# Window attention, depthwise and quantised convolutions: band matrices by DMA, weights quantised beside the first bands, halved sums of exponentials, projections one step later

## The chip, the cores and the metric

The kernel runs on one core of one Trainium2 chip. The metric is the device time of one execution in microseconds. TensorE (PE in the profile) multiplies, ScalarE (ACT) applies functions, VectorE (DVE) and GpSimd (POOL) work elementwise, and SyncE (SP) issues the DMAs. Each engine works through its own instructions in order.

## The reference

Two layers on `x` of 4 x 128 channels x 128 x 128, all in float32. Layer 0 cuts each image into 9 x 9 overlapping windows of 16 x 16 pixels (step 14), and runs attention with 4 heads of 32 channels in each:

```python
y = _ln(tok, ln1_g, ln1_b)
q, k, v = split(y @ w_qkv)                       # per head
attn = softmax(q @ k.T * hd ** -0.5)
tok = (attn @ v) @ w_out + b_out + tok
merged = scatter_add(tok) / count                # back to the image, overlaps averaged
y = _ln(xf, ln2_g, ln2_b) @ w_p0 + b_p0          # 128 -> 256 channels
ym = depthwise_conv5x5(y, dw_k)                  # 256 channels, padding 2
ym = gelu(gelu(batchnorm(ym)))
x1 = ym @ w_p2 + b_p2 + xf
```

Layer 1 is a residual block with quantised activations (4 bits, 0 to 1) and quantised weights (4 bits, scaled by the largest absolute weight):

```python
out = conv3x3(act_quant(x1), weight_quant(w1)); out = batchnorm(out)
out = conv3x3(act_quant(out), weight_quant(w2)); out = batchnorm(out)
return out + x1
```

## The kernel before

**Preparation.** Weights are loaded, and the gains and biases of the layer norms are folded into them. Lines 165 to 196 bound the largest attention score from the weights and set `flag`; a second, safe version of all layers runs only if `flag` is set, which it is not here. Lines 202 to 224 load both 3x3 weights, find the largest absolute value (VectorE, then a reduction over partitions on POOL) and write them as fp8. Lines 229 to 279 make the matrices of the depthwise convolution. The 5x5 convolution runs on TensorE as a product over 40 rows (20 image rows by even and odd pixels) with a banded matrix per channel, in three shifts `s` and 32 outputs `m`. For each of the 96 pairs of shift and output, VectorE copies a picked pattern twice (L264), TensorE multiplies it with the taps (L269), and VectorE and ScalarE copy the result into `wst` (L277, L275). Eight DMAs store `wst` in `dw_d` (L279), from which the loop loads 768 KB a time into `w` (L471).

**Band loop.** A band is 16 image rows of one image; there are 9 an image, 36 in all (t = 0 to 35). The order of TensorE, ScalarE and VectorE is the order in which the program is written; SP and POOL are ordered by the scheduler. For band t the loop runs over its 9 regions j (windows side by side). `scores(j)`: 8 products into `sc` (L561), and two exponentials into `pt` (L569). Then `values(j-1)`: 8 products of `pt` with `v`, and 8 with a block of `ones`, which gives the sums of the exponentials in the same shape (L615); VectorE takes the reciprocal (L628) and multiplies (L630, L632); POOL adds the seam between regions (L635). A float32 product counts as two passes in the profile, so the 16 products are 32 passes.

**Side work.** `beside(t)` writes a list of steps for each band, which is laid evenly between the regions, a half of a region at a time, with `values_in(j)` (L549) between the halves:
- `one`, the layer norm and q/k projections of band t+1, four chunks of 4, 4, 4 and 2 rows (4 in the first band of an image). A chunk has four steps: head (centring product L306, square L308), tail (variance product L313, `rstd` L315 and L316, `xn` on VectorE L318, copy to `yr` on POOL L378), and the projections to q and k (L382).
- `two`, the output side of band t-1, four chunks with five steps: project (product with `wo` L420, `xf` on VectorE L423), head, tail, and the two products with `wp0` (L437) whose results go to `y2_d` (L451). Before the first of them, `post_begin` averages the seams on POOL (L404, L405, L407).
- convolution steps of an earlier half image, 16 for each of 8 units; four go beside a band where there are any. A step is 96 passes (L496), two copies on ScalarE (L505), four statistics on VectorE (L507) and four stores to `cv_d` (L511).

In `beside`, the index c counts the chunks, and chunk c of `one` stands beside chunk c of `two`. All PSUM tiles of the side work come from `ps_m`, three banks; `po` has one.

**After the loop.** Half an image of convolution is left, then the batch norm's statistics (L746 on), the Gelu and first 3x3 convolution pass, a second pass, and a last pass that writes the output.

Of the kernel before, what the change touches and what calls it, by code (L numbers as in the profile page):

```python
# [8 lines left out]
F32 = mybir.dt.float32  # L9
# [5 lines left out]
P = 128  # L15
# [17 lines left out]
CW = P // 2 + 2  # L33
NCK = 8
# [7 lines left out]
def layers(  # L42
# [47 lines left out]
    dw_d = dram.tile([NCK, P, 16 * 3 * 32], F32, name="dw_d")  # L90
# [37 lines left out]
    bng, bnb = vector(bn_g, "bng"), vector(bn_b, "bnb")  # L128
    wp2 = const.tile([P, 2, P], F32, name="wp2")
    nc.sync.dma_start(out=wp2, in_=w_p2.rearrange("(h p) m -> p h m", p=P))  # L130
    bp2 = vector(b_p2, "bp2")
    ga1, be1 = vector(gamma1, "ga1"), vector(beta1, "be1")
    ga2, be2 = vector(gamma2, "ga2"), vector(beta2, "be2")

# [4 lines left out]
    with (  # L139
# [25 lines left out]
        if not safe:  # L165


            sq = prep.tile([P, 2 * P], F32, name="sq")
            nc.vector.tensor_tensor(sq, wqkv[:, : 2 * P], wqkv[:, : 2 * P], ALU.mult)
            all1 = prep.tile([P, P], F32, name="all1")  # L170
            nc.vector.memset(all1, 1.0)
            pn = ps_p.tile([P, 2 * P], F32, name="pn")
            nc.tensor.matmul(pn, all1, sq, start=True, stop=True)
            norm = prep.tile([P, 2 * HEADS], F32, name="norm")
            nc.vector.tensor_reduce(
                norm, pn.rearrange("p (h d) -> p h d", d=HD), AX.X, ALU.add
            )
            mask = prep.tile([P, HEADS], F32, name="mask")
            nc.vector.tensor_reduce(
                mask, ident.rearrange("p (h d) -> p h d", d=HD), AX.X, ALU.add  # L180
            )
            qb2 = prep.tile([P, 1], F32, name="qb2")
            nc.vector.tensor_tensor(qb2, qb, qb, ALU.mult)
            nc.vector.tensor_scalar(mask, mask, qb2, None, ALU.mult)
            pq = ps_p.tile([P, HEADS], F32, name="pq")
            nc.tensor.matmul(pq, all1, mask, start=True, stop=True)

            bound = prep.tile([P, HEADS], F32, name="bound")
            nc.vector.tensor_scalar(bound, norm[:, :HEADS], float(P), None, ALU.mult)
            nc.vector.tensor_tensor(bound, pq, bound, ALU.add)  # L190
            nc.vector.tensor_tensor(bound, bound, norm[:, HEADS:], ALU.mult)
            top = prep.tile([P, 1], F32, name="top")
            nc.vector.tensor_reduce(top, bound, AX.X, ALU.max)
            nc.vector.tensor_scalar(
                flag, top[0:1, :], MAX_SCORE**2 / (2.0 * P), None, ALU.is_ge
            )

    wq, kscale = [], []
    with tc.tile_pool(name=f"wprep_{tag}", bufs=2) as wprep:
        for n, w in enumerate((w1, w2)):
            wf = wprep.tile([P, 9 * P], F32, name="wf")
            nc.sync.dma_start(out=wf, in_=w)
            am = wprep.tile([P, 1], F32, name="am")
            nc.vector.tensor_reduce(am, wf, AX.X, ALU.max, apply_absolute_value=True)
            alpha = wprep.tile([P, 1], F32, name="alpha")
            nc.gpsimd.partition_all_reduce(alpha, am, P, bass_isa.ReduceOp.max)  # L210
            nc.vector.tensor_scalar(alpha, alpha, 1e-12, None, ALU.add)
            ks = const.tile([P, 1], F32, name=f"kscale{n}")
            nc.vector.tensor_scalar(ks, alpha, 1.0 / 105.0, None, ALU.mult)
            ra = wprep.tile([P, 1], F32, name="ra")
            nc.vector.reciprocal(ra, alpha)
            nc.vector.tensor_scalar(wf, wf, ra, 1.0, ALU.mult, ALU.min)
            nc.vector.tensor_scalar(wf, wf, -1.0, 7.0, ALU.max, ALU.mult)
            nc.vector.tensor_scalar(wf, wf, ROUND, None, ALU.add)
            q = const.tile([P, 9, P], F8, name=f"wq{n}")
            nc.vector.tensor_scalar(  # L220
                q.rearrange("p t o -> p (t o)"), wf, ROUND, None, ALU.subtract, saturate=False
            )
            wq.append(q)
            kscale.append(ks)

# [3 lines left out]
    with (  # L231
        tc.tile_pool(name=f"dwp_{tag}", bufs=1) as dwp,
        tc.tile_pool(name=f"ps_w_{tag}", bufs=4, space=PSUM) as ps_w,
    ):
        zero = dwp.tile([P, 2 * 2 * 2 * CW], F32, name="zero")
        nc.gpsimd.memset(zero, 0.0)
        for b in range(B):
            for d in (y2_d[b][0][0:2], y2_d[b][NU - 1][UR + 2 :]):
                nc.sync.dma_start(
                    out=d.rearrange("r e c x -> (r e c x)").rearrange("(p n) -> p n", p=P), in_=zero  # L240
                )
        dwk = dwp.tile([P, 2, N_TAPS], F32, name="dwk")
        nc.sync.dma_start(out=dwk, in_=dw_k.rearrange("(h p) o i j -> p h (o i j)", p=P))
        pk = ps_w.tile([P, 2 * P], F32, name="pw")
        for h in range(2):
            nc.tensor.transpose(pk[:N_TAPS, h * P : (h + 1) * P], dwk[:, h, :], ident)
        taps = dwp.tile([N_TAPS, 2 * P], F32, name="taps")
        nc.vector.tensor_copy(taps, pk[:N_TAPS])

        pick = dwp.tile([N_TAPS, 35, 7], F32, name="pick")  # L250
        nc.gpsimd.memset(pick, 0.0)
        for k in range(N_TAPS):
            dy, dx = divmod(k, 5)
            nc.vector.tensor_copy(pick[:, dy + 15, dx + 1 : dx + 2], ident[:N_TAPS, k : k + 1])
        wst = dwp.tile([P, NCK, 16, 3, 32], F32, name="wst")
        ms = [dwp.tile([N_TAPS, 2, 32, 2], F32, name=f"m{n}") for n in range(4)]
        for m in ms:
            nc.gpsimd.memset(m, 0.0)
        for n in range(3 * 32):
            s, ro, eo = n // 32, n % 32 // 2, n % 2  # L260
            m = ms[n % 4]
            for half in range(2):

                nc.vector.tensor_copy(  # L264
                    m[:, half, : GR + 4, :],
                    pick[:, 15 - ro : 15 - ro + GR + 4, 2 * s - eo + 1 : 2 * s - eo + 3],
                )
            pw = ps_w.tile([P, 2 * P], F32, name="pw")
            nc.tensor.matmul(pw, m.rearrange("t a r e -> t (a r e)"), taps, start=True, stop=True)  # L269
            for half in range(2):  # L270
                hs = slice(64 * half, 64 * half + 64)
                o = wst[hs, :, :, s, 2 * ro + eo]
                i_ = pw[hs].rearrange("p (k a c) -> p k a c", k=NCK, a=2)[:, :, half, :]
                if half:
                    nc.scalar.copy(o, i_)  # L275
                else:
                    nc.vector.tensor_copy(o, i_)  # L277
        for k in range(NCK):
            nc.sync.dma_start(out=dw_d[k], in_=wst[:, k].rearrange("p c s m -> p (c s m)"))  # L279
# [7 lines left out]
    with ExitStack() as actx:  # L287
# [6 lines left out]
        small = pool("small", 6)  # L294
        ps_s, ps_o, ps_m = (pool(n, k, space=PSUM) for n, k in (("ps_s", 1), ("ps_o", 1), ("ps_m", 3)))

        xb, yr, qs, kr, ob = {}, {}, {}, {}, {}

        def normalise(src, n):
# [11 lines left out]
            def tail():  # L311
                pv = ps_m.tile([P, 512], F32, name="pm")
                nc.tensor.matmul(pv[:, :n], avg, held["sq"][:, :n], start=True, stop=True)  # L313
                rstd = work.tile([P, 512], F32, name="rstd")
                nc.scalar.activation(rstd[:, :n], pv[:, :n], AF.Ln, bias=eps_t)  # L315
                nc.scalar.activation(rstd[:, :n], rstd[:, :n], AF.Exp, scale=-0.5)  # L316
                xn = work.tile([P, 512], F32, name="xn")
                nc.vector.tensor_tensor(xn[:, :n], src(), rstd[:, :n], ALU.mult)  # L318
                return xn
# [143 lines left out]
        def conv_steps(n):  # L463
# [4 lines left out]
            def load(k):  # L468
                ut = up.tile([P, 4, 16, CW], F32, name="u")
                wt = up.tile([P, 16, 3, 32], F32, name="w")  # L470
                nc.sync.dma_start(out=wt.rearrange("p c s m -> p (c s m)"), in_=dw_d[k])  # L471
                for half in range(2):
                    ch = 32 * k + 16 * half
                    for a, z in ((0, GR), (GR, GR + 4)):
# [12 lines left out]
            def pair(k, jj):  # L487
                ut, wt = U[k]
                pc = [ps_m.tile([P, 2, 256], F32, name="pm") for _ in range(2)]
                for j in range(2):  # L490
                    for s in range(3):
                        for half in range(2):
                            hs = slice(64 * half, 64 * half + 2 * GR + 8)
                            for q in range(4):
# [5 lines left out]
                                    wt[hs, c, s, :], ut[hs, :, c, s : s + 64],  # L500
# [30 lines left out]
        def attention(t):  # L531
# [39 lines left out]

            def scores_safe(j):
# [35 lines left out]
            def values(j):  # L608
                pt, v = S.pop(("pt", j)), S.pop(("v", j))
                po = ps_o.tile([P, 2, NT], F32, name="po")  # L610
                for m in range(1 if safe else 2):
                    for kc in range(2):
                        for h in range(HEADS):
# [19 lines left out]
                if j:  # L633
                    seam = o[:, :, j * STEP : j * STEP + 2]
                    nc.gpsimd.tensor_tensor(seam, seam, part, ALU.add)  # L635

            begin()
            return scores_safe if safe else scores, values_in, values

        def beside(t):  # L640

# [328 lines left out]
```

## Time and profile before

| | us |
|---|---|
| median of 3 runs (4049.6 to 4061.1) | 4058.78 |
| the profiled execution: time | 4057.53 |
| the profiled execution: span, first to last instruction | 4055.7 |
| first attention scores start | 168.6 |
| second band's scores start | 217.5 |
| the band loop ends | about 2830 |
| last unit of the convolution | 2830 to 2985 |

All views come from one profiled execution. A group's row reads: line, engine, operation, output from input, shapes, count; then busy time in us and the mean duration of one in ns; then the idle time of the engine just before them and what ended it. A timeline's row gives start and duration in us. A wait's row reads: engine, line, what it waited for, total us, number, longest.

### The profile page before, as it was taken

How to read it: one execution, taken by the hardware profiler on the slowest of the kernel's cores; microseconds unless marked ns; L12 is line 12 of the kernel's file. 1: busy time of each engine (PE TensorE's matmuls, PEld its weight loads, DVE VectorE, ACT ScalarE, POOL GpSimd, SP SyncE). 2: the span in 40 equal slices, each digit the busy share in tenths (PEclk: the TensorE clock that was granted, in tenths of full speed). 3: DMA queues.
4: the chain of work that ended last, by engine and by line, in shares of the span. 5: the costliest groups of instructions: out<-in, count | busy, mean ns of one | idle time of the engine just before them, and what ended most of it. 6: DMA issues, size and time to landing. Idle time of an engine off the chain costs nothing.

```text
span 4055.7 us, 87210 instructions
## 1 busy us (share of the span) xinstructions
PE 3762.9 (93%) x35916; PEld 1914.1 (47%) x35916; DVE 1826.5 (45%) x3358; ACT 2326.4 (57%) x3534; POOL 384.2 (9%) x1381
## 2 busy tenths in 40 slices
PE   7699999999999999999999999997688889999999
PEld 5355455555555555555545555553333333334444
DVE  5244444444444444444444444442245555685433
ACT  3367666666666666666666666653156667662233
POOL 0011110111110010111110111100011111100000
PEclk9999999999999999999999999998579999999999
DMA  1223266676656657655666764657888889760487
GB/s 39 108 62 80 73 135 149 146 143 152 148 116 141 148 134 159 150 140 110 150 147 139 160 146 118 144 129 162 182 255 300 295 297 304 231 199 1 137 271 250
DMA packets 782938, 643.68 MB, mean 159 GB/s; under 512 B 572736, under 2 KB 585664, under 8 KB 782528
## 3 DMA queue, kind: packets, MB, share of 16 engines
q1 hardware_dynamic: 782528, 637.98, 60.8%
q8 instruction: 286, 4.69, 0.5%
q14 instruction: 124, 1.02, 0.1%
HBM read 365.07 MB, written 272.76 MB: 157 GB/s over the span
## 4 chain that ended last, share of the span: by engine, by line
PE 76%; DMA 9%; ACT 4%; issue 3%; DVE 3%; POOL 2%; SPq 2%; ACTq 0%; POOLq 0%; DVEq 0%
PE po L615 14%; PE pc L787 12%; PE pm L496 9%; PE sc L561 8%; PE pm L306 6%; PE pm L382 6%; PE pm L313 6%; PE pm L437 5%; DMA cv<-cv_d 3%; PE pm L549 3%; PE pb L849 3%; PE pm L420 2%; PE pw L269 2%; DMA c1l<-c_d 2%; DMA u<-y_d 2%
## 5 line engine op out<-in xcount | busy, mean ns | idle before, releaser
L628 DVE RECIPROCAL rd<-po 128x256 f32<-128x256 f32 x324 | 569.6, 1758 | 633.4 <-PE po L615 633.4
L787 PE MATMUL pc<-q,wq 128*128 128x512 fp8e4 x3456 | 794.5, 382 | 23.3 <-DVE st L794 9.4
L569 ACT ACTIVATE pt<-sc 128x1024 f32<-128x1024 f32 x648 | 627.2, 1019 | 58.0 <-PE sc L561 47.1
L787 PEld LDWEIGHTS <-wq 128*128 128x128 fp8e4 x3456 | 337.4, 98 | 517.5 <-issue 151.6
L496 PE MATMUL pm<-u,w 40*32 40x256 f32 x12288 | 454.6, 410 | 57.4 <-DMA u<-y_d 44.7
L507 DVE BATCH_NORM_STATS2 st<-c 128x6 f32<-128x256 f32 x512 | 181.4, 414 | 469.4 <-ACT c L505 468.9
L561 PE MATMUL sc<-q,kr 32*128 32x256 f32 x5184 | 373.6, 401 | 0.0
L496 PEld LDWEIGHTS pm<-u,w 40*32 40x32 f32 x12288 | 258.7, 112 | 240.8 <-issue 112.2
L505 ACT COPY c<-pm 128x512 f32<-128x512 f32 x256 | 139.0, 588 | 386.8 <-PE pm L496 377.8
L615 PE MATMUL po<-pt,v 128*32 128x256 f32 x5184 | 346.9, 385 | 0.0
L615 PE MATMUL po<-pt,ones 128*32 128x256 f32 x5184 | 339.1, 379 | 0.0
L561 PEld LDWEIGHTS sc<-q,kr 32*128 32x128 f32 x5184 | 233.9, 184 | 218.7 <-issue 181.3
L313 PE MATMUL pm<-sq,avg 128*128 128x512 f32 (+1 forms) x576 | 281.9, 571 | 31.7 <-ACT sq L308 27.0
L443 ACT ACTIVATE y<-pm,bp 128x512 f32<-128x512 f32 (+1 forms) x288 | 183.4, 641 | 222.9 <-PE pm L437 111.9
L849 PE MATMUL pb<-ge,wp 128*128 128x512 f32 x512 | 265.6, 614 | 46.6 <-ACT ge L846 46.5
L382 PE MATMUL pm<-xn,wqkv 128*128 128x512 f32 (+1 forms) x576 | 269.2, 570 | 15.6 <-DVE xn L318 15.6
L437 PE MATMUL pm<-xn,wp 128*128 128x512 f32 (+1 forms) x576 | 268.9, 559 | 5.7 <-DVE xn L318 5.7
L841 ACT ACTIVATE ge<-cv,shift,scale 128x512 f32<-128x512 f32 x256 | 202.8, 844 | 111.2 <-DMA cv<-cv_d 107.2
L308 ACT ACTIVATE sq<-pm 128x512 f32<-128x512 f32 (+1 forms) x288 | 157.2, 546 | 187.8 <-PE pm L306 187.7
L794 DVE BATCH_NORM_STATS2 st<-pc 128x6 f32<-128x512 f32 x256 | 177.8, 696 | 189.3 <-PE pc L787 189.2
L918 ACT ACTIVATE z<-pc,shift,scale 128x512 f32<-128x512 f32 x128 | 99.3, 777 | 269.0 <-PE pc L787 130.1
L315 ACT ACTIVATE rstd<-pm,eps_t 128x512 f32<-128x512 f32 (+1 forms) x288 | 184.3, 640 | 120.3 <-PE pm L313 114.7
(143 smaller groups left out, 4026.0 us busy)
## 6 DMA issues: line engine op xcount, KB each, us to landing
u<-y_d SPq DMA_DIRECT2D x128, 528.0 KB
cv_d<-c SPq DMA_DIRECT2D x512, 128.0 KB
cv<-cv_d SPq DMA_DIRECT2D x128, 512.0 KB
y_d<-y SPq DMA_DIRECT2D x224, 264.0 KB
w<-dw_d SPq DMA_DIRECT2D x64, 768.0 KB
xfl<-xf_d SPq DMA_DIRECT2D x128, 256.0 KB
id_d<-y SPq DMA_DIRECT2D x128, 256.0 KB
idt<-id_d SPq DMA_DIRECT2D x128, 256.0 KB
```

The source lines that it names most:

```text
L306: nc.tensor.matmul(pc[:, :n], center, src(), start=True, stop=True)
L313: nc.tensor.matmul(pv[:, :n], avg, held["sq"][:, :n], start=True, stop=True)
L382: nc.tensor.matmul(pm[:, : n * P], wqkv[:, m * P : (m + 1) * P], held["xn"][:, : n * P], start=True, stop=True,)
L437: nc.tensor.matmul(pm[:, : n * P], wp0[:, h, :], held["xn"][:, : n * P], start=True, stop=True)
L496: nc.tensor.matmul(pc[half][32 * q : 32 * q + 32, j, :].rearrange("p (g x) -> p g x", g=4), wt[hs, c, s, :], ut[hs, :, c, s : s + 64], sta ...
L561: nc.tensor.matmul(sc[h // 2][:, h % 2, kc, :].rearrange("p (r c) -> p r c", c=RS), region(kr, j)[hs, kc * P : (kc + 1) * P], queries(j, h ...
L569: nc.scalar.activation(pt, sc[p], AF.Exp)
L615: nc.tensor.matmul(po[hs, m, :], ones if m else v[:, kc, hs], pt[h // 2][:, h % 2, kc, :], start=(kc == 0), stop=(kc == 1),)
L628: nc.vector.reciprocal(rd, po[:, 1, :])
L787: nc.tensor.matmul(pc, w[:, t, :], q[:, k * RB + dy : k * RB + dy + RB, dx : dx + P], start=(t == 0), stop=(t == 8),)
L841: nc.scalar.activation(ge[:, h, :].rearrange("p (r c e) -> p r e c", r=RB, e=2), cv[:, h, :].rearrange("p (r e c) -> p r e c", r=RB, e=2), ...
L849: nc.tensor.matmul(pb, wp2[:, h, :], ge[:, h, :], start=(h == 0), stop=(h == 1))
```

## The change

It has five parts.

1. The banded matrices are made without TensorE. The taps are loaded transposed, element by element (25 x 256), and written into a zeroed array `pad_d` in DRAM; 32 copies from DRAM to DRAM cut the shifted patterns into `band_d`; six times, SP loads a part (40 x 32 x 128), POOL reorders it, and SP stores it in `dw_d`. The tiles that this needs are borrowed from the pool of the `u` tiles (two buffers).
2. The weights are quantised in 14 steps that are put into the list of side work, four beside each of the first bands; the tiles are borrowed from the same pool, after the band matrices.
3. VectorE adds the two halves of each pair of exponentials (`halves(j)`, after `values(j-1)`), and 4 instead of 8 products with `ones` are made per region.
4. In `beside`, chunk c of `two` stands beside chunk c+1 of `one`; there is one more round (n is 5 instead of 4).
5. Smaller ones: `rstd` is written over `sq`; `w` is loaded for 2 x 40 rows instead of 128; some vectors and `wp2` are loaded after the band matrices' first DMAs; the bound on the scores is computed after the loop, at the batch norm's statistics.

```diff
-    dw_d = dram.tile([NCK, P, 16 * 3 * 32], F32, name="dw_d")
+    dw_d = dram.tile([2 * NCK, KD, 3, 16 * 32], F32, name="dw_d")
+    pad_d = dram.tile([2 * GR + 3, 7, 2 * P], F32, name="pad_d")
+    band_d = dram.tile([32, 3, KD, 2 * P], F32, name="band_d")
...
+        def band_matrices():
...
+            taps = scratch(2 * P)[:N_TAPS]
+            nc.sync.dma_start(out=taps, in_=dw_k.rearrange("c o i j -> (o i j) c"))
...
+            for dy in range(5):
+                nc.sync.dma_start(out=pad_d[GR - 1 + dy, 1:6, :], in_=taps[5 * dy : 5 * dy + 5, :])
+            for ro in range(GR):
+                for eo in range(2):
+                    nc.sync.dma_start(
+                        out=band_d[2 * ro + eo].rearrange("s (r e) c -> s r (e c)", e=2),
+                        in_=bass.AP(
+                            pad_d.tensor,
+                            pad_d[GR - 1 - ro, 1 - eo, 0:1].offset,
+                            [[4 * P, 3], [7 * 2 * P, GR + 4], [1, 4 * P]],
+                        ),
+                    )
+            for c in range(0, 2 * P, 128):
+                for s in range(3):
+                    by_m = scratch(32 * 128)[:KD].rearrange("p (m c) -> p m c", m=32)
+                    nc.sync.dma_start(
+                        out=by_m, in_=band_d[:, s, :, c : c + 128].rearrange("m p c -> p m c")
+                    )
+                    by_c = scratch(32 * 128)[:KD]
+                    nc.gpsimd.tensor_copy(
+                        by_c.rearrange("p (c m) -> p m c", m=32), by_m
+                    )
+                    nc.sync.dma_start(
+                        out=dw_d[c // 16 : (c + 128) // 16, :, s, :].rearrange("k p n -> p k n"),
+                        in_=by_c.rearrange("p (k n) -> p k n", n=16 * 32),
+                    )
+        def quantised(n, w):
...
+            return [load, largest, scales, clip, widen, to_int, to_f8]
...
-                rstd = work.tile([P, 512], F32, name="rstd")
+                rstd = held["sq"]
...
+            def halves(j):
+                S["sm", j] = []
+                for p in range(2):
+                    sm = sums.tile([P, 2, NT], F32, name=f"sm{p}")
+                    pt = S["pt", j][p]
+                    nc.vector.tensor_tensor(sm, pt[:, :, 0, :], pt[:, :, 1, :], ALU.add)
+                    S["sm", j].append(sm)
...
-                for m in range(1 if safe else 2):
-                    for kc in range(2):
-                        for h in range(HEADS):
-                            hs = slice(h * HD, (h + 1) * HD)
-                            nc.tensor.matmul(
-                                po[hs, m, :], ones if m else v[:, kc, hs], pt[h // 2][:, h % 2, kc, :],
-                                start=(kc == 0), stop=(kc == 1),
-                            )
+                for kc in range(2):
+                    for h in range(HEADS):
+                        hs = slice(h * HD, (h + 1) * HD)
+                        nc.tensor.matmul(
+                            po[hs, 0, :], v[:, kc, hs], pt[h // 2][:, h % 2, kc, :],
+                            start=(kc == 0), stop=(kc == 1),
+                        )
+                if not safe:
+                    sm = S.pop(("sm", j))
+                    for h in range(HEADS):
+                        hs = slice(h * HD, (h + 1) * HD)
+                        nc.tensor.matmul(
+                            po[hs, 1, :], ones, sm[h // 2][:, h % 2, :], start=True, stop=True
+                        )
...
+            lag = 1 if one else 0
+            n = max(len(one), len(two) + lag, 1)
...
+                second = two[c - lag] if 0 <= c - lag < len(two) else [None] * 5
+                before = two[c - lag - 1] if 0 <= c - lag - 1 < len(two) else [None] * 5
+                steps += [first[0], second[0], before[3], *conv_of[2 * c], first[1], second[1], before[4]]
+                steps += [*conv_of[2 * c + 1], second[2], first[2], first[3]]
...
-        todo, share = [], [0]
+        todo, share = [], [4]
+        for n_, w in enumerate((w1, w2)):
+            todo += quantised(n_, w)
...
                     scores(j)
                     if last:
                         last()
+                    halves(j)
```

## The prediction

> **What bounds the kernel now.** I read the page's busy times first, then busy time by stretch, then the chain of waits, then the timeline of single regions. The page gives the engine that is full and the rows that the change touches.
>
> ```profile
> PE 3762.9 (93%) x35916; PEld 1914.1 (47%) x35916; DVE 1826.5 (45%) x3358; ACT 2326.4 (57%) x3534; POOL 384.2 (9%) x1381
> L615 PE MATMUL po<-pt,ones 128*32 128x256 f32 x5184 | 339.1, 379 | 0.0
> L628 DVE RECIPROCAL rd<-po 128x256 f32<-128x256 f32 x324 | 569.6, 1758 | 633.4 <-PE po L615 633.4
> ```
>
> Busy time by stretch (TensorE first, then weight loads, VectorE, ScalarE): in a stretch inside the band loop TensorE is busy 97% at full clock, the others are far from it. The loop runs from 168.6 us to about 2830 us; a piece that leaves TensorE there is worth its own length, as long as nothing new makes TensorE wait.
>
> ```profile
> 2000.00:2600.00 600.00, 580.65 (x7047) 311.26 (x7044) 263.40 (x418) 378.53 (x596) 64.73 (x270) 1.00 0.62 141
> ```
>
> The waits of TensorE are short, about 2.2 us a band: one wait for the squares and one for POOL's seam work before the first projection by `wo`.
>
> ```profile
> PE pm L420 <- POOL ob L407: 50.7, 32, 4.5
> PE pm L313 <- ACT sq L308: 27.0, 40, 0.7
> ```
>
> Ahead of the loop stands a preparation that TensorE, VectorE and ScalarE do in lockstep (chain of waits: start, length):
>
> ```profile
> 30.95 82.27 PE pw L269 x192
> 120.97 10.07 DMA dw_d<-wst
> ```
>
> One region on the timeline (start, length), which gives all the offsets below:
>
> ```profile
> 778.21 1.15 PE L561 MATMUL sc<-q,kr 32*128 32x256 f32 x16
> 779.28 1.07 PE L615 MATMUL po<-pt,v 128*32 128x256 f32 x16
> 780.17 1.05 PE L615 MATMUL po<-pt,ones 128*32 128x256 f32 x16
> 781.15 1.12 PE L420 MATMUL pm<-ob,wo 128*128 128x512 f32 x2
> 781.28 1.76 DVE L628 RECIPROCAL rd<-po 128x256 f32<-128x256 f32 x1 [1.76 <-PE po L615]
> 783.48 0.74 DVE L423 SCALAR_TENSOR_TENSOR xf<-pm,bo,xr 128x512 f32<-128x512 f32 x1
> ```
>
> With S the start of the scores (778.21): side work starts at S+2.94, the reciprocal at S+3.07, VectorE is free for side work at S+5.27, `xf` is there at S+6.0. A 512-wide product of the side work takes 0.86 (0.96 as the first after another shape), a 256-wide one 0.43, the values' projection 0.44, a convolution step 3.2.
>
> **Halved sums.** Of 16 passes over `ones` per region 8 go. 32 passes of L615 take 1.86 us (779.28 to 781.15, less the 0.1 of the switch), so 8 take 0.485, and 324 regions give 157 us of TensorE time. For it VectorE gets two 128x512 sums per region. The trace has such an operation, the product `xn` at 0.69 us; two in a row take 1.3 us, 421 us in all, on an engine with the room for it (263 of 600 us busy). But the place matters: they stand in VectorE's queue behind the reciprocal and its two products and before all side work. The reciprocal now starts at S+2.6 and is done with its products at S+4.8; the exponentials are ready at S+3.1; the sums end at S+6.1; then come `xf` (S+6.9) and `xn`. What is queued behind them: TensorE's centring product, which needs `xf`, and the products that need `xn`. Side work now starts at S+2.46.
>
> **One step later.** At the start of a band the side work is head, variance and two q/k projections of the next band; the projection by `wo` that stood between them leaves. At the end of a band the last two 256-wide `wp0` products directly follow their variance product. I went through the nine regions in the built order of instructions.
>
> Region 0: head S+2.46, variance S+4.27 (waits for the squares, as now), values' projection to S+5.7. From the variance product to the projection of its `xn` takes 3.35 us in this trace:
>
> ```profile
> 843.91 1.13 PE L313 MATMUL pm<-sq,avg 128*128 128x512 f32 x2 [0.69 <-ACT sq L308]
> 845.38 1.12 PE L420 MATMUL pm<-ob,wo 128*128 128x512 f32 x2
> 847.26 1.12 PE L382 MATMUL pm<-xn,wqkv 128*128 128x512 f32 x2 [0.76 <-DVE xn L318]
> ```
>
> So the projection starts at S+7.6, after a wait of 1.9 us, and the region takes 9.5 us (9.16 to 9.45 now). The POOL wait goes, and this wait is late next. Region 2 of a band with convolution: head and variance are adjacent, 0.8 us for the squares. Region 3 of such a band, and regions 1, 3 and 7 of one without: projection by `wo` and centring now fall into one region with only 2.3 us of products between; `xf` comes at S+6.9 and is wanted at S+5.6, so 1.3 us (1.9 in region 7). Region 8: variance (256 wide) to S+3.9, values to S+4.3; its `xn` is behind the sums and ready at S+6.6, so 2.3 us. The waits of a band add up to 7.3 us.
>
> Adding products, steps and waits, a band with convolution takes 76.1 us (now 75.5 from one first variance product to the next, 613.84 to 689.34) and one without 65.4 (now 62.5). 27 bands by +0.6 are +16, eight by +2.9 are +23 us. So the 157 us are given back in waits. The offsets carry perhaps 1 us a band either way, so the loop lies between about -10 and +75 us.
>
> **Band matrices by DMA.** The 96 products with their 384 copies go, and what lies before the first scores (168.6 us). In their place SP issues a chain of DMAs, and in SP's queue behind it stand the loads of band 0's third and fourth row blocks and of the following bands. Taps: 6400 single elements. The nearest row is a `cv_d` store of 512 pieces of 256 B, which the chain shows landing in up to 4.4 us; the first weight load shows that some 2.1 of it is latency (issued by 1.14, its reader starts at 3.23). 12.5 times 2.1 to 4.4 is 26 to 55 us; I take 38, nearer the low end because the pieces are smaller. SP reaches it at 7.4 us, behind nine loads and two row blocks; the padding's stores and their landing add 5.5. The 32 band copies go eight at a time: 32 issues of 0.44 us are 14 us; four rounds of the slowest landing in the trace (10.07) are 40. I take 40, since rows of 20 by 3 are far from the 128 of every row here. All bands have then landed at 91 us (53 to 108), T below. Only then are the first reordering load and the missing row blocks issued (landing T+6); two blocks take 20 us as now (134.3 to 154.2), so the first scores come at T+26.
>
> The page counts short packets:
>
> ```profile
> DMA packets 782938, 643.68 MB, mean 159 GB/s; under 512 B 572736, under 2 KB 585664, under 8 KB 782528
> ```
>
> Without the 262,144 of `cv_d` and 270,336 of `y_d`, 40,256 are left: 256 rows of taps, 2048 single vector elements, 16 for each of 2308 DMAs, and 8 for each of the 128 `u` loads of 8 rows. The Trainium skill's "DMA: Bandwidth & Descriptors", section "Why a DMA increments its semaphore by 16 and not by 1", says that a DMA runs on the largest number of engines up to 16 that divides the outermost size of both sides, which fits the 8. By it the band copies (3 outermost) run on 3 engines: an estimate of 57 us, from the 6.3 MB in 17 us that `dw_d` had on 16, and the sum would be 17 us more.
>
> Then six rounds of load, POOL copy, store. A POOL copy of 4096 elements at L378's 1.15 ns is 4.7 us, a load some 5.5 (between `wf` at 3.87 and 11 at the `cv_d` rate), 11 us a round. In POOL's queue copies three and four stand behind seam work of regions 1 and 3, so they run at T+44 and T+56; the last ends at T+83, and only then does a buffer come free for the quantised weights, landing at T+87. Band 0's VectorE queue has the largest-value step at region 4, T+55: it waits about 33 us there, and everything behind it, TensorE through `sm` too. With its 49 us (168.6 to 217.5) band 0 ends at T+26+49+33+2 = T+110 = 201, now 217.5: -16 us (-54 with the lower T; +25 with T of 108 and loads of 9.5 us). The 134 us of preparation are thus nearly all replaced by waits.
>
> **The rest.** Quantising beside bands puts nine steps of 0.7 to 1.35 us (rows L208, L216) into VectorE's queue: +4 with band 0's sums. The score bound moves to the batch norm after the loop, beside the 2.8 us of Gelu work that follow: +1. `w` in two smaller loads (64 more issues of 0.33 us on SP, spread over the loop) and `rstd` in `sq` (free again once `xn` is made, two buffers later): 0, hidden by TensorE's products; TensorE waits in the loop for neither. The last unit's 150 us stay bound by `u` loads and 256-byte stores.
>
> **Sum.** The profiled execution took 4057.5 us (span 4055.7), 1.3 below the median of 4058.8. -16 +16 +23 +4 +1 = +28: 4086. With the ends of loop and preparation combined, not all at their worst, this case spans 4030 to 4145. About 0.3% (12 us) is what a measurement can tell from no change.
>
> **Rivals.**
>
> TensorE's saving comes through: the extra VectorE work hides and the late steps find cover. For: VectorE is under half busy. Against: the 0.76 us wait above is there already with a product in between. In full: 4057.5-157-16+5 = 3890, chance 0.07. With half of the 36 times 7.3 us of waits gone it is 131 us less, 3955, with a quarter 4020: chance 0.15 for this middle ground.
>
> Slower by the preparation: single elements or band copies on few DMA engines. If T is 150, VectorE's wait at region 4 ends at 237 and the sum is 4145. It decides from T of about 110 on. Chance 0.13.
>
> Loop and preparation cancel, within 12 us: 0.12. That the change doesn't do what it says I give nothing: the built order has the 2592 passes fewer.
>
> My forecast, above 4070, has 0.53; what its span has below that is counted in the two cases before.
>
> The range, 4010 to 4150, leaves out the full saving and the far end of the slow preparation. Faster 0.22, same 0.12, slower 0.66.
>
> **What would show it.** After: 2592 passes over `ones`, 648 sums near 0.69 us; TensorE's wait for POOL gone from the `wo` product; new waits of `wqkv` products for `xn` near 1.9 us once a band, of `wp0` products for `xn` near 2.3, of centring for `xf` near 1.3; bands at 76 and 65 us. In band 0 the step on the largest weight waits for its DMA for some 30 us, and the second band starts near 201 us. If the loop's bands come out under 74 us, or those three waits stay under 3 us a band in sum, I am wrong.

## Result and the profile after

The change makes the kernel slower: 4203.9 us (median of 4 runs, 4199.5 to 4214.1) against 4054.7 in the same session, a ratio of 1.0374 with a 95% interval of 1.0352 to 1.0396. The forecast was 4086 with a range to 4150. The profiled execution of the changed kernel has a span of 4212.3 us, 156.6 more than before (4055.7).

First the rows that answer to those of before: the engines' busy times, the groups of the halved sums, the reciprocal, and the stretch 2000 to 2600 us.

```profile
PE 3659.8 (87%) x33130; PEld 1801.2 (43%) x33130; DVE 2192.3 (52%) x3692; ACT 2290.9 (54%) x3438; POOL 545.3 (13%) x1382
```
```profile
L613 PE MATMUL po<-sm,ones 128*32 128x256 f32 x2592 | 205.3, 387 | 1.7 <-DVE sm L560 1.7
L560 DVE TENSOR_TENSOR sm<-pt 128x512 f32<-128x512 f32 x648 | 445.4, 728 | 6.2 <-ACT pt L551 6.2
L625 DVE RECIPROCAL rd<-po 128x256 f32<-128x256 f32 x324 | 569.3, 1757 | 726.8 <-PE po L613 726.6
```
```profile
2000.00:2600.00 600.00, 550.93 (x6366) 286.76 (x6354) 334.99 (x540) 356.95 (x563) 85.66 (x243) 0.96 0.61 132
```

The passes over `ones` are 2592 fewer and the 648 sums take 0.728 us each. TensorE only waits 1.7 us for the sums themselves. Yet in the stretch it is busy for 551 of 600 us instead of 581, and its granted clock, the third figure from the end, is 0.96 instead of 1.00. Both are new. Its waits over the whole execution (engine, tile, line, what it waited for: total us, number, longest):

```profile
PE pm L361 <- DVE xn L297: 137.6, 40, 57.6
PE pm L416 <- DVE xn L297: 80.7, 39, 2.6
...
PE pm L292 <- ACT sq L287: 46.4, 67, 1.0
PE pm L285 <- DVE xf L402: 45.5, 50, 4.1
...
PE pm L399 <- POOL ob L386: 10.1, 2, 5.2
```

The wait for POOL before the product with `wo` (50.7 us before) is nearly gone; the products that need `xn` or `xf` wait instead. (The longest wait, 57.6 us, lies in the first band; from the second band on none is longer than 2.8 us until the last band starts.) On TensorE's timeline, from the end of the band that starts at 968.6 us over the start of the next one (start, length, in brackets the idle time before), it can be seen what such a wait does:

```profile
1041.27 0.61 PE L531 MATMUL pm<-wqkv,yr 128*128 128x128 f32 x4
1044.03 1.13 PE L416 MATMUL pm<-xn,wp 128*128 128x256 f32 x4 [2.15 <-DVE xn L297]
1045.09 3.08 PE L478 MATMUL pm<-u,w 40*32 40x256 f32 x96
...
1052.42 1.12 PE L292 MATMUL pm<-sq,avg 128*128 128x512 f32 x2 [0.69 <-ACT sq L287]
1053.38 0.61 PE L531 MATMUL pm<-wqkv,yr 128*128 128x128 f32 x4
1055.95 3.24 PE L361 MATMUL pm<-xn,wqkv 128*128 128x512 f32 x4 [1.96 <-DVE xn L297]
1059.12 1.53 PE L543 MATMUL sc<-q,kr 32*128 32x256 f32 x16
```

The four passes of L361 behind the wait of 1.96 us take 3.24 us; the same four take 1.88 us elsewhere in the loop (at 1014.56). The trace's records of the granted clock say why: from 1056.5 to 1059.9 us TensorE ran at half clock. Such a stretch mostly lasts 3.41 us or two or three times that. In bands 1 to 34 of the changed kernel (a band here runs from its first scores to those of the next) they add up to 202 us in 34 stretches, before to 7.

The first bands, as the DMA queue, POOL and VectorE show them:

```profile
21.15 2.34 SPq L208 DMA_DIRECT2D pad_d<-u  x5
...
25.63 44.27 SPq L212 DMA_DIRECT2D band_d<-pad_d  x32
...
80.01 0.32 SPq L223 DMA_DIRECT2D u<-band_d  x1
...
155.29 0.29 SPq L230 DMA_DIRECT2D dw_d<-u  x1
155.62 0.40 SPq L223 DMA_DIRECT2D u<-band_d  x1
...
174.94 0.29 SPq L230 DMA_DIRECT2D dw_d<-u  x1
```
```profile
167.79 7.12 POOL L227 COPY u<-u 40x4096 f32<-40x4096 f32 x1 [12.53 <-DMA u<-band_d]
```
```profile
201.70 1.35 DVE L251 TENSOR_REDUCE am<-u 128x1 f32<-128x1152 f32 x1 [54.88 <-DMA u<-in_L_conv_w_dram]
```

The band copies have landed at 80.0 us, the first scores start at 107.9. From store to store a round of load, reordering and store takes 19.7 us: 12.2 from the load's issue to the copy's start, 7.1 for the copy. VectorE waits 54.9 us for the first 3x3 weight, and the second band's scores start at 223.9 (before at 217.5).

So the 156.6 us lie as follows: +6.4 up to the second band, +141.1 in bands 1 to 34 (2625.7 against 2484.6), +9.1 after the start of the last band. That last stretch, to which the change adds only the last band's sums and the score bound, was between 1341 and 1363 us in all kernels of this study; I take no cause for it.

### The profile page after: what moved, and what is told of

It is laid out like the page before. It is cut to its first block, busy times and chain, and to the rows that moved or that the text cites. A ratio compares the mean times of both kernels' runs of the same rounds, so it can differ in the third digit from the quotient of the medians.

```text
span 4212.3 us, 82324 instructions
## 1 busy us (share of the span) xinstructions
PE 3659.8 (87%) x33130; PEld 1801.2 (43%) x33130; DVE 2192.3 (52%) x3692; ACT 2290.9 (54%) x3438; POOL 545.3 (13%) x1382
## 5 line engine op out<-in xcount | busy, mean ns | idle before, releaser
L478 PE MATMUL pm<-u,w 40*32 40x256 f32 x12288 | 472.8, 439 | 62.3 <-DMA u<-y_d 51.4
L560 DVE TENSOR_TENSOR sm<-pt 128x512 f32<-128x512 f32 x648 | 445.4, 728 | 6.2 <-ACT pt L551 6.2
L543 PE MATMUL sc<-q,kr 32*128 32x256 f32 x5184 | 398.2, 423 | 0.1
L361 PE MATMUL pm<-xn,wqkv 128*128 128x512 f32 (+1 forms) x576 | 274.9, 590 | 137.6 <-DVE xn L297 137.6
L478 PEld LDWEIGHTS pm<-u,w 40*32 40x32 f32 x12288 | 274.8, 119 | 246.6 <-issue 134.2
L605 PE MATMUL po<-pt,v 128*32 128x256 f32 x5184 | 361.5, 398 | 0.3 <-DVE part L629 0.3
L416 PE MATMUL pm<-xn,wp 128*128 128x512 f32 (+1 forms) x576 | 281.7, 582 | 80.7 <-DVE xn L297 80.7
L543 PEld LDWEIGHTS sc<-q,kr 32*128 32x128 f32 x5184 | 247.7, 195 | 219.8 <-issue 184.5
L632 POOL TENSOR_TENSOR ob<-ob,part 128x32 f32<-128x32 f32 x288 | 172.2, 598 | 833.7 <-DVE part L629 819.2
L294 ACT ACTIVATE sq<-pm,eps_t 128x512 f32<-128x512 f32 (+1 forms) x288 | 183.7, 638 | 150.8 <-PE pm L292 149.1
```

The source lines that it names most:

```text
L361: nc.tensor.matmul(pm[:, : n * P], wqkv[:, m * P : (m + 1) * P], held["xn"][:, : n * P], start=True, stop=True,)
L416: nc.tensor.matmul(pm[:, : n * P], wp0[:, h, :], held["xn"][:, : n * P], start=True, stop=True)
L478: nc.tensor.matmul(pc[half][32 * q : 32 * q + 32, j, :].rearrange("p (g x) -> p g x", g=4), wt[hs, s, c, :], ut[hs, :, c, s : s + 64], sta ...
L543: nc.tensor.matmul(sc[h // 2][:, h % 2, kc, :].rearrange("p (r c) -> p r c", c=RS), region(kr, j)[hs, kc * P : (kc + 1) * P], queries(j, h ...
L560: nc.vector.tensor_tensor(sm, pt[:, :, 0, :], pt[:, :, 1, :], ALU.add)
L605: nc.tensor.matmul(po[hs, 0, :], v[:, kc, hs], pt[h // 2][:, h % 2, kc, :], start=(kc == 0), stop=(kc == 1),)
```

## The experiments

Two theories were set against each other: that the loop loses by waits and by the clock that follows them, made by halved sums and later step together; and that VectorE's queue or the new preparation is to blame alone. The parts were taken apart first. In the diffs `-` is the kernel named in the expectation, `+` the experiment. Times are medians; ratios, to the kernel before in the same session (its median was 4037 to 4055), are what is compared.

**Halved sums alone.**

```diff
+            def halves(j): ...                  # sums on VectorE, 4 products with ones
...
-                rstd = work.tile([P, 512], F32, name="rstd")
+                rstd = held["sq"]
```

> The kernel before with the halved sums alone (order of the side work and preparation as before). Theory, clock: the loss of the change comes in the loop from waits of about 2 us that halved sums and the later step make together, each followed by a stretch of 3.4 to 10 us at half the TensorE clock (202 us of such stretches in bands 1 to 34 of the changed kernel, 7 before). With the old order the projection by wo stands between a variance product and the product that needs its xn, so few waits reach 2 us, less than 60 us of half clock in the loop, and most of the 137 us that the eight passes are worth remain: 3930 to 4010 us, bands with convolution near 73.5 us. Rival, VectorE's queue: the sums delay xf and xn by 1.3 us a region wherever the side work stands; then the waits are there without the later step too, and the time is 4080 or more.

(`rstd` is written over `sq` too, here and in the next.) Measured: 3981.2 us, ratio 0.9854 (0.9836 to 0.9873). Faster, as the first theory had it; conv bands (bands with convolution) 74.1 us in the mean (76.1 before; without bands 6, 15, 24 and 33, the first after a pause of the convolution, here and below), half clock 61 us in bands 1 to 34, just over the 60 expected. VectorE's queue alone does not make the loss.

**Halved sums and later step, old preparation.**

```diff
+            def halves(j): ...
+            lag = 1 if one else 0
```

> The kernel before with halved sums and the later step; preparation as before. Clock theory: bands 1 to 34 take 2600 to 2640 us as in the changed kernel (2626), and only the first band's 6 us and the end's few are taken back: 4180 to 4200 us. Rival, preparation: the new preparation carries the loss, and without it the time is 4060 to 4100.

Measured: 4187.7 us, 1.0367 (1.0338 to 1.0396), bands 1 to 34 in 2612.7 us. The loss is there without the new preparation.

**The changed kernel without the later step.**

```diff
-            lag = 1 if one else 0
+            # order of steps as in the kernel before
```

> The changed kernel with the side work in the old order (halved sums and new preparation stay). Clock theory: as the halves alone plus some 10 us of the new preparation, 3940 to 4020 us. Rival, VectorE's queue: 4100 to 4200, as the waits for xf and xn stay without the later step. Rival, preparation: over 4100 too, but with bands under 75 us.

Measured: 3996.1 us, 0.9899 (0.9875 to 0.9922). Taking the later step out turns 3.7% slower into 1.0% faster.

**The changed kernel without halved sums.**

```diff
-                            po[hs, 1, :], ones, sm[h // 2][:, h % 2, :], start=True, stop=True
+                                po[hs, m, :], ones if m else v[:, kc, hs], pt[h // 2][:, h % 2, kc, :],
```

> The changed kernel with 16 passes over ones in every region again, and no sums on VectorE (later step and new preparation stay). Clock theory: xf and xn come 1.3 us earlier, the waits of TensorE in a band fall from 7.2 to about 3 us and none reaches 2 us, so the half clock goes from the loop (under 60 us): bands with convolution near 77 us, time 4080 to 4120, faster than the changed kernel although TensorE has 2592 passes more. Rival, waits without a clock: 142 us of passes back, 140 us of waits gone, 4190 to 4210.

Measured: 4165.2 us, 1.0314 (1.0292 to 1.0335), between the range of the clock theory and that of the rival; conv bands 79.2 us. Half of my expectation failed. The half clock is gone from bands 1 to 34 (0 us), and with 2592 passes more the kernel is faster than the changed one: TensorE is busy only 29 us longer there (rows below), though the passes of these bands are worth 133 (worked out further down). But I had the waits at 3 us a band, and they are 5.2. The later step waits without any sums on VectorE:

```profile
PE pm L361 <- DVE xn L297: 59.1, 34, 2.0
PE pm L416 <- DVE xn L297: 45.4, 34, 1.8
PE pm L292 <- ACT sq L287: 42.6, 62, 0.7
```

The first of them is as long as with the sums (61.9 us in these bands): the way from a variance product over ScalarE and VectorE to the projection of its `xn` takes 3.35 us, and the later step took away the product that stood in it.

**The new preparation alone.**

```diff
+        band_matrices()                         # and quantised(...), the late score bound, w in two loads
             # no halves(j), no lag: as in the kernel before
```

> The kernel before with the new preparation alone (band matrices by DMA, quantising beside the first bands, score bound late), no halved sums, old order of the side work. Theory: the 134 us of preparation are replaced by waits of the same length, second band within 6 us of 217 us: 1.000 to 1.006 of before. Rival, preparation as a gain: second band near 200 and 0.996 or less. With e4 it gives the later step by itself: about 100 us.

Measured: 4051.6 us, 1.0034 (1.0021 to 1.0046); second band at 221.7 us. It costs a little, and is not the cause.

The stretches from the second band's scores to the last band's in five of these kernels. The columns are the stretch, its length, the busy time of TensorE, weight loads, VectorE, ScalarE, POOL, then TensorE's clock, and the DMAs' share and GB/s; length less TensorE's time is its idle time. Before:

```profile
217.50:2702.10 2484.60, 2404.13 (x28349) 1287.71 (x28348) 1088.60 (x1708) 1579.19 (x2487) 272.64 (x1136) 1.00 0.59 133
```

New preparation alone, then with halved sums, then with the later step, then with both (the changed kernel):

```profile
221.70:2697.70 2476.00, 2401.92 (x28345) 1287.30 (x28344) 1094.10 (x1720) 1578.02 (x2487) 275.83 (x1137) 1.00 0.56 128
```
```profile
222.90:2641.00 2418.10, 2298.19 (x25901) 1219.41 (x25900) 1477.93 (x2334) 1579.47 (x2487) 385.99 (x1137) 0.99 0.59 131
```
```profile
220.60:2805.90 2585.30, 2409.97 (x28349) 1282.37 (x28348) 1091.72 (x1720) 1574.65 (x2487) 274.93 (x1137) 1.00 0.53 122
```
```profile
223.90:2849.60 2625.70, 2381.22 (x25901) 1238.33 (x25900) 1476.43 (x2334) 1579.95 (x2487) 387.64 (x1139) 0.96 0.56 120
```

| bands 1 to 34, us | length | TensorE busy | idle | at half clock |
|---|---|---|---|---|
| preparation alone | 2476.0 | 2401.9 | 74.1 | 0 |
| and halved sums | 2418.1 | 2298.2 | 119.9 | 58 |
| and later step | 2585.3 | 2410.0 | 175.3 | 0 |
| and both | 2625.7 | 2381.2 | 244.5 | 202 |

Halved sums bring 58 us, the later step costs 109; if they only added up, both together would cost 51. They cost 150. Of the 98 too many, 23 are idle time beyond the sum of the two, and the half clock is 144 us longer than the sum, worth half of that, 72; some 3 us are left over.

**Keeping TensorE busy.** That the clock is a cost of its own needs a run in which waits are filled, not shortened.

```diff
-                for c in range(2):
+                for c in [0, 1] * (5 if j in (0, 8) else 1):
                     nc.tensor.matmul(pv[:, c, :], ...)      # values_in
```

> The changed kernel, in which the values' projection of regions 0 and 8 of each band is made five times instead of once (the same products into the same tile, 8 x 0.44 us more for TensorE a band, 127 us in all), so that TensorE has products where it waited for xn 1.8 and 2.2 us. Clock theory: the waits are only filled, not shortened, so the added products cost about nothing, and the half clock of bands 1 to 34 falls from 202 to under 60 us, which is worth about half of the difference: 4110 to 4160 us, faster than the changed kernel with more work in it. Rival, waits alone: no gain, 4190 to 4230.

Measured: 4114.4 us, 1.0188 (1.0167 to 1.0210). With 127 us more of products the kernel is faster by 1.9% of before (1.0374 less 1.0188), some 75 us. (This is the fifth run that later expectations speak of.)

```profile
222.20:2756.00 2533.80, 2415.38 (x26987) 1323.73 (x26987) 1472.95 (x2330) 1587.31 (x2487) 392.49 (x1135) 1.00 0.55 125
```

Bands 1 to 34 are 91.9 us shorter. The added products, 120 us of the 127 in these bands, stand in place of 126 us of idle time (244.5 to 118.4), so the two nearly cancel; the half clock fell from 202 to 17 us, and half of these 185 is 92.5. TensorE's busy time grew by 34 us where 120 were added, which gives 86. The clock alone is some 86 to 92 us of the change's loss.

**How much filling it needs.** In the changed kernel's trace I cut the whole execution into windows of 3.41 us along the edges of the clock's records. Of the windows at full clock in which TensorE was busy less than 40%, all 25 were followed by half clock; between 40 and 45% it was 15 of 18, between 45 and 60% 7 of 44, above that none of 975. A wait of some 1.9 us in one window would then be the point. The kernel without halved sums agrees: in its bands 1 to 34 no window at full clock is under 45%, 35 are between 45 and 60%, and none is followed by half clock. Next the fifth run's kernel with the projection made three times instead of five:

```diff
-                for c in [0, 1] * (5 if j in (0, 8) else 1):
+                for c in [0, 1] * (3 if j in (0, 8) else 1):
```

> As the fifth run, but with the values' projection of regions 0 and 8 made three times instead of five (63 us of added products instead of 127). The two waits for xn of 1.8 and 2.2 us then shrink to about 0.9 and 1.3 us and stay. Threshold theory (TensorE's clock halves after a window of 3.4 us that is less than about 0.45 busy, that is, with more than some 1.9 us of waiting in it): both waits are under it, the half clock of bands 1 to 34 stays under 40 us, and the time is that of the fifth run, 4105 to 4125 us. Rival (every microsecond of waiting costs clock in proportion): half of the fifth run's gain, half clock near 110 us, 4150 to 4165.

Measured: 4121.6 us, 1.0194 (1.0177 to 1.0211), the fifth run's time within the intervals; half clock 24 us. The waits for `xn` stay, each under the point:

```profile
PE pm L416 <- DVE xn L297: 43.7, 33, 1.4
...
PE pm L361 <- DVE xn L297: 32.6, 34, 1.1
```

So what a wait costs in clock rises steeply near one length, and not in proportion to it: half the filling brought all of the gain.

**Towards a better kernel.** Without the later step the one large wait left is the old one, for POOL (first row: bands 1 to 34 of the run without it; second: with the preparation alone).

```profile
PE pm L399 <- POOL ob L386: 69.8, 34, 2.6
```
```profile
PE pm L399 <- POOL ob L386: 35.5, 30, 1.2
```

A convolution step can be put in front of it.

```diff
-            conv_of = [conv[len(conv) * c // (2 * n + 2) : ...] for c in range(2 * n + 2)]
+            conv_of = [conv[0:1]] + [conv[1:][(len(conv) - 1) * c // (2 * n + 1) : ...] for c in range(2 * n + 1)]
```

> The changed kernel without the later step (3996 us in its run), with the first convolution step of a band moved to the band's start, between the head and the variance product of the next band's first row block. The two waits of region 0 (for POOL before the projection by wo, 2.05 us a band, and for the squares, 0.69) get 3.2 us of products. Theory: in 26 bands with convolution some 2.5 us of waiting go, and the half clock that follows them: 3900 to 3945 us. Rival: the step is missed where it was taken from, and POOL's wait moves with it: 3980 to 4010.

Measured: 3948.0 us, 0.9773 (0.9753 to 0.9793), just above the range. Most conv bands take 69.4 us, 4.7 less than the mean before; but bands 10, 19 and 28, in each of which a convolution unit starts, take 85.5 to 85.7, since the step now comes at once after the issue of its own loads:

```profile
830.24 1.08 PE L478 MATMUL pm<-u,w 40*32 40x256 f32 x8 [7.77 <-DMA u<-y_d]
835.07 5.34 PE L478 MATMUL pm<-u,w 40*32 40x256 f32 x88 [3.76 <-DMA u<-y_d]
```

Each of the three also holds 17.1 us of half clock, worth half of that; most other conv bands of this run hold none.

And the preparation can stand beside the bands with its DMAs, not only with its quantising:

```diff
-        todo, share = [], [4]
+        todo, share = band_matrices(), [7]      # now a list of 23 steps, the 14 of quantising behind them
-        band_matrices()
```

> The changed kernel without the later step (3996 us), with the DMAs and copies of the band matrices made as steps beside bands 0 to 3, and the quantising after them, seven steps a band; they no longer stand in SP's queue ahead of band 0's row blocks. Theory (queue): first scores near 30 us instead of 108, VectorE's wait of 55 us for the weights gone, the second band near 85 instead of 223: 3850 to 3885 us. Rival (contention): copies on POOL and 44 us of DMA issue on SP hold back the first bands, half of the gain comes back as waits there: 3910 to 3940.

Measured: 3901.1 us, 0.9648 (0.9623 to 0.9672), between the theory's range and the rival's. The scores of the first and second band:

```profile
40.05 1.51 PE L559 MATMUL sc<-q,kr 32*128 32x256 f32 x16
```
```profile
96.60 1.15 PE L559 MATMUL sc<-q,kr 32*128 32x256 f32 x16
```

The second band starts 126 us earlier than without the spreading (222.9); bands 1 to 3 take 73.0, 79.1 and 64.3 us instead of about 61, so some 33 us of the gain come back there, as the rival had it in part.

**Both.**

```diff
+            fresh = t < 6 or (t >= 2 and bands[t - 2][1] in (4, NR - 1))
+            k = 0 if fresh else 1               # first step to the front, but not where a unit starts
```

> The two gains together: preparation beside the bands (3901 us alone) and the convolution step first in the band (conv bands 69.4 instead of 74.1 us), except in the first band of a convolution unit, where the step's own loads are not there yet (those bands took 75 to 86 us with the step first, with waits for u of up to 7.8 us). 21 or 22 bands of 4.2 to 4.7 us less: 3800 to 3820 us, 0.94 of before. If the waits for u were not the cause of the long bands, bands 10, 19 and 28 stay near 85 us, and the time is 3830 to 3850.

Measured: 3876.1 us, 0.9558 (0.9535 to 0.9581): the best kernel of the study, 4.4% faster than before, but 56 us above my range (some 38 by the ratio: the kernel before took 4055 us when it was measured beside this one, and 4037 beside the two parts). Bands 10, 19 and 28 are short now (72 to 73 us), so the loads of `u` were their cause; but bands 11, 20 and 29 became the long ones (83 to 84):

```profile
807.38 7.23 SPq L509 DMA_DIRECT2D cv_d<-c  x4
814.95 5.87 SPq L329 DMA_DIRECT2D xr<-in_x_dram  x1
```
```profile
824.26 2.05 PE L301 MATMUL pm<-xf,center 128*128 128x512 f32 x2 [11.30 <-DVE xf L418]
```

The load of `xr` stands in SP's queue behind the stores of the step that was moved, and its own issue takes 5.87 us, where the others beside it take some 0.4; why, no run shows. TensorE waits 11.3 us for the `xf` made with it, and each of these bands holds 13.7 us of half clock. It was not tried to mend this.

## Why the prediction went wrong, step by step

The direction was right, the size was not: +28 us were forecast, +149 measured in the medians.

- **The waits: right in sum.** 7.3 us a band were forecast; bands 1 to 34 have 244.5 / 34 = 7.2. The three kinds named, in these bands:

```profile
PE pm L416 <- DVE xn L297: 73.6, 34, 2.6
PE pm L361 <- DVE xn L297: 61.9, 34, 2.0
...
PE pm L285 <- DVE xf L402: 40.4, 48, 2.2
```

The projection in region 0 was forecast at 1.9 us and waits 61.9 / 34 = 1.8; `wp0` in region 8 at 2.3, and 73.6 / 34 = 2.2. The centring for `xf` was forecast at 1.3 and more and waits 40.4 / 48 = 0.84 each time; short waits that I had not listed (for `y`, 23 us in all) make up for a part of that, so the close sum is partly luck. My condition for being wrong, under 3 us, did not come: the three together are 5.2 us a band.
- **What a wait costs: wrong, and the largest error.** The step that failed is "adding products, steps and waits": it took each wait for its own length, with the products behind it at full clock. I had read "97% at full clock" of before and carried the clock over. The trace of before had it to show: its bands 6 and 24 hold one half-clock stretch each and take 79.0 and 78.0 us, bands 15 and 33 with the same work 77.0 and 77.2. The plain bands without half clock (3 and 32) took 65.8 and 65.9 us, as forecast (65.4); those with one stretch of 3.4 us took 67.4 to 67.6, the conv bands 80.4 in the mean against a forecast 76.1. With the clock held up (the fifth run) conv bands take 77.0. Over bands 1 to 34 the 195 us more of half clock are 98 us, which no term of the sum held, and no end of the range. The Trainium skill's "TensorE: Matmul & The Clock Gate", section "Part 1: The HAM clock gate", gives a window of 3413 ns, after which an idle TensorE runs at half clock; the stretches of 3.41 us and its multiples agree with the window. Its advice to avoid gaps of over some 3 us (section "Why this matters for your kernels") does not reach: no wait of TensorE in bands 1 to 34 was longer than 2.8 us, and 15 of the 18 windows that were 40 to 45% busy were still followed by half clock. The measurement decides.
- **Eight passes fewer: 0.485 us forecast, 0.44 measured.** From the start of the values' products to the next group it was 1.87 us (779.28 to 781.15) and is now 1.43:

```profile
999.87 1.07 PE L605 MATMUL po<-pt,v 128*32 128x256 f32 x16
...
1001.30 1.12 PE L399 MATMUL pm<-ob,wo 128*128 128x512 f32 x2
```

My 0.485 does not follow from its own row: 1.87 less the 0.1 of the switch is 1.77, and a quarter of that is 0.44. From preparation alone to halved sums TensorE's busy time fell by 103.7 us, and 29 of half clock are in it: 133 for 306 regions, 0.43. My 157 us for 324 regions should have been 141.
- **Who makes the waits: not asked.** The forecast took the sums and the later step as one. The runs separate them: the later step alone adds 101 us of waits in bands 1 to 34, the sums alone 46, mostly at the old place before `wo`. The rival "TensorE's saving comes through", which I gave 0.07 in full, and 0.15 in part, describes, in its partial form, the sums without the later step (ratio 0.985), not the change.
- **Preparation: -16 forecast, second band 23 us later than that.** Two errors partly cancelled before T: the taps, 38 us in the sum, were there within 14 (issue at 7.2, the stores that read them at 21.2), and the band copies took 54 instead of 40 (25.6 to 80.0; the issue alone 44.3, at 1.2 us each in the median). The estimate of 57 that the forecast drew from the Trainium skill's "DMA: Bandwidth & Descriptors", section "Why a DMA increments its semaphore by 16 and not by 1", came closer, but that may be luck: 44 of the 54 us are SP's issuing, which it does not hold, and no run shows on how many engines the copies ran. T was 80 instead of 91. Behind it a round took 19 to 22 us where I had 11: the copy of 40 x 4096 takes 7.1 to 7.3 us (I took 4.7 from a copy of another shape), and a load 12.2. So the weights came at 201.7 instead of 178, and VectorE waited 55 instead of 33 us. The rival "slower by the preparation" (T of 110 and more) did not come true; its time of 4145 was nearest to the result for another reason.
- **The sum.** Forecast to the profiled execution: second band +23 us, bands 1 to 34 +102 (141 against 39), the rest +4: 28 + 129 = 157.

The range was too narrow because its upper end added only terms of the same kind: offsets of waits, and T. A state of the engine that follows from the waits had no term. (The lower end of the loop, -10, does not follow from the 1 us a band either way that the forecast names: 39 less 36 is +3.)

## What to carry to other kernels

A wait of TensorE is not worth its length alone: in this kernel one near 2 us could halve the clock of the products behind it for 3.4 us or more, so waits are to be kept short one by one, and a long one is better split by any product that can be moved into it. Before two changes are costed together, ask which of the new waits each makes alone: here one part gained 1.5%, the other lost nearly 3%, and together they lost more than the sum. DMAs of a preparation belong beside the work that does not need them yet, step by step, and not ahead of it in the one queue that also loads the first tiles.

## What the runs showed of the hardware that was not expected

- TensorE's granted clock fell to half after windows of 3.41 us that were busy under about 40 to 45%, and never (0 of 975) after windows that were busy over 60%; a busy window did not always bring it back at once (of 97 windows at half clock that were over 80% busy, 51 were followed by another).
- Adding 127 us of products that change nothing made the kernel some 75 us faster.
- A load of 6400 single elements of 4 bytes landed within 14 us, beside the padding's store (issued at 7.2, the store that reads it at 21.2).
- SP needed 44.3 us to issue 32 copies from DRAM to DRAM (0.66 to 2.3 us each), where its loads of rows took 0.3 to 0.5.
